# Two-layer graph kernel: the scaled and split diffusion rows of a block moved to the next pair's first attention groups

## The chip, the cores and the metric

The kernel runs on one core of a Trainium2 chip. The metric is the device time of one launch in microseconds. The engines are TensorE (PE in the profile; its weight loads are PEld), VectorE (DVE), ScalarE (ACT), GpSimd (POOL) and SyncE (SP, which here only issues DMAs). Each has its own queue of instructions.

## The reference

Two layers over 2708 nodes with 512 features. The first is a graph attention layer. The second layer, cut to what matters here:

```python
def _adj_from_feats(Xa, W1, W2, W3):
    logits = (Xa @ W1) @ W2 @ (Xa @ W3).T
    # keep, in each row, the fewest largest softmax shares that sum to 0.9
    masked = jnp.where(keep, logits, -jnp.inf)
    return jax.nn.softmax(masked, axis=1)

S = S + eye(n)
Rf = S / S.sum(axis=1, keepdims=True)
Rb = S / S.sum(axis=0)[:, None]
Xf = Xb = Xa = X
Z = 0
for s in range(2):
    A = _adj_from_feats(Xa, W1, W2, W3)
    Xf = Rf @ Xf
    Xb = Rb @ Xb
    Xa = A @ Xa
    Z = Z + (Xf @ U1[s] + Xb @ U2[s] + Xa @ U3[s])
Y = layernorm(X + Z) * gamma + beta
```

In the first step Xf and Xb start from the same X, so that S @ X is computed once; its rows are scaled by the row sums for Xf and by the column sums for Xb.

## The kernel before, in words

Rows are cut into 22 tiles of 128 (the last has 20 rows), two tiles make a pair (11 pairs), four make a quad (6 quads, the last of two tiles). After the first layer the loop `for s in range(STEPS)` does the two steps of the second. Within a step `for g in range(-1, NP)` goes over the pairs, and in one turn of it several pieces of work of different pairs stand side by side:

- **Logits** of pair g + 2 (`Logits.products`, L521): 24 matmuls into PSUM, and ACT copies the 12 chunks into `p` (L523), which has four buffers, those of two pairs.
- **Their exponentials** (`Logits.exp`): the row maxima on DVE (L548), and then 19 small steps, the list `fills`: for each tile two passes of ACT over a row (L553 with half the exponent, L560 in place), then a step of POOL that sets three first points (L565 to L575), an empty step, 12 "looks" (L553: each a pass of ACT over a row) and a last POOL step that makes masses of them.
- **The search** of pair g + 1 (`search`), on DVE: a prologue (L624 to L653), two rounds (L629), then `finish`, which writes `keep` (L806, L808, L730) and ends in a branch (L890). `early` is called behind the first round, and brings the row maxima of pair g + 2; `late` is called ahead of `finish`, and brings the rest of pair g's own work.
- **Attention** of pair g (`attended`): `keep` is transposed on PE in groups of four chunks (L1016), copied by ACT (L1020, tile `at`, two buffers) and multiplied with the values (L1035). A tile has six groups, five of four chunks and one of two, so a pair has twelve, counted by n. The copy of group n + 1 stands ahead of group n's matmuls. From `n >= first` on, which is 3 and in pair 0 is 7, each group also takes steps of `fills` (two up to n = 8, then one), and every group takes steps of `others`.
- **Mixing** of pair g (`mixed`, L1076): the products with U1, U2, U3, each in four k steps, which also take one step of `others` each and, in the first two of them, one of `fills` in three k steps.

The list `others` is what `part` returns. It is the product S @ X for a quad, cut in two: an even g brings the first 11 of the 22 chunks of its sum and an odd g the other 11 (`product`, L967, with the loads of `hl`, three buffers, and `s_r`). With the second half, in the first step, `part` adds eight `scaled` steps, two for each tile of the quad (L977): ACT scales the PSUM tile q into `xe` (four buffers), POOL stores it to `xfb_d` (L978), and `split_rows` splits it on DVE into a high and a low part (L181, L182; tile `split_hl`, two buffers), which POOL stores to `fhl_d` or `bhl_d` (L183). The last quad, of two tiles, has four such steps.

Pair g loads its rows of Xf and Xb from `xfb_d` with `diffused` (L1001, on SP's queue), a step that is put into `others`.

PE, ACT, DVE and SP run their instructions in the order in which the program writes them (`tc.manual_schedule`); POOL's order is the scheduler's. For an odd pair in the first step, the eight scaled steps come last in `others`, so they fall into the groups from n = 8 on and into the first k step of `mixed`, and in DVE's queue they stand between the two rounds of the search of pair g + 1 and its `finish`:

```python
late()
finish(0)
```

In pair 0 the eight scaled steps of quad 0 were left over from the turn before (`left`), and stand ahead of its attention.

Of the kernel before, what the change touches and what calls it, by code (L numbers as in the profile page):

```python
# [53 lines left out]
def kernel(  # L54
# [37 lines left out]
    pairs = [list(range(g, min(g + G, NT))) for g in range(0, NT, G)]  # L92
# [17 lines left out]
    fhl_d = dram.tile([NT * P, 2, D], F32, name="fhl_d")  # L110
    bhl_d = dram.tile([NT * P, 2, D], F32, name="bhl_d")
# [13 lines left out]
    rinv = const.tile([P, NT], F32, name="rinv")  # L125
    cinv = const.tile([P, NT], F32, name="cinv")
# [787 lines left out]
    for s in range(STEPS):  # L914
        last = s == STEPS - 1
        with ExitStack() as st:
# [18 lines left out]
            def values():  # L935
                for t in range(NT):
                    nc.sync.dma_start(out=va[:rows[t], t, :], in_=(xa_d if last else va_d)[cols[t], :])
# [5 lines left out]
            def part(half, b):  # L943

                if b // 2 >= len(quads):
                    return []
                quad = quads[b // 2]  # L950
                first = b % 2 == 0
                w = len(quad) * P
                hl_d = (fhl_d if first else bhl_d) if last else vhl_d
                cs = range(NT) if last else range(0, NT // 2) if first else range(NT // 2, NT)
                steps = []

                def product(c):
                    if c == 0:
                        half[:] = [ps_s.tile([P, D], F32, name=f"q{i}") for i in range(len(quad))]
                    hl = sp.tile([P, 2, D], F32R, name="hl", bufs=3)  # L960
                    nc.sync.dma_start(out=hl.bitcast(F32), in_=hl_d[c * P:(c + 1) * P])
                    s_r = sp.tile([P, 2 * G * P], F32R, name="s_r")
                    nc.sync.dma_start(out=s_r[:, :w].bitcast(F32),
                                      in_=s_d[c * P:(c + 1) * P, quad[0] * P:quad[0] * P + w])
                    for j in range(len(quad)):
                        for h in range(2):
                            nc.tensor.matmul(half[j], lhsT=s_r[:, j * P:(j + 1) * P], rhs=hl[:, h],  # L967
                                             start=(c == 0 and h == 0), stop=(c == NT - 1 and h == 1))

                def scaled(t, ps, i, inv, to):  # L970
                    pr = rows[t]

                    if last and b < 2 and t % 2:
                        x = work.tile([P, D], F32, name="xw", bufs=2)
                    else:
                        x = work.tile([P, D], F32, name="xe", bufs=2 if last else 4)
                    nc.scalar.activation(x[:pr], ps[:pr], AF.Copy, scale=inv[:pr, t:t + 1])  # L977
                    nc.gpsimd.dma_start(out=xfb_d[i, cols[t], :], in_=x[:pr])  # L978
                    if not last:
                        split_rows(parts, nc.vector, x[:pr], t, to)  # L980

                steps += [lambda c=c: product(c) for c in cs]
                if last or not first:
                    for j, t in enumerate(quad):
                        if first or not last:
                            steps.append(lambda j=j, t=t: scaled(t, half[j], 0, rinv, fhl_d))
                        if not first:
                            steps.append(lambda j=j, t=t: scaled(t, half[j], 1, cinv, bhl_d))
                return steps

            def paced(steps, n):
                for step in steps[:n]:
                    step()
                del steps[:n]

            def diffused(grp):
                out_ = []
                for i in range(2):
                    for t in grp:
                        x = work.tile([P, D], F32, name=f"x{i}")  # L1000
                        nc.sync.dma_start(out=x[:rows[t]], in_=xfb_d[i, cols[t], :])  # L1001
                        out_.append(x)
                return out_[:len(grp)], out_[len(grp):]

            def attended(grp, keep, rden, fills, others, then, first=3):

                def turned(i, t, cs):
                    pr = rows[t]
                    pt = ps_t.tile([P, TG, P], F32, name="t")
                    at = work.tile([P, TG, P], F32, name="at")
                    for j, c in enumerate(cs):
                        nc.tensor.transpose(pt[:rows[c], j, :pr], keep[i][:pr, cols[c]], ident[:pr, :pr])  # L1016
                    full = sum(rows[c] == P for c in cs)
                    for r, j0, j1 in ((P, 0, full), (rows[cs[-1]], full, len(cs))):
                        if j0 < j1:
                            nc.scalar.copy(at[:r, j0:j1, :pr], pt[:r, j0:j1, :pr])  # L1020
                    return at

                steps = [(i, t, cs) for i, t in enumerate(grp) for cs in tgroups]
                at = turned(*steps[0])
                xa = []
                total = len(others)
                for n, (i, t, cs) in enumerate(steps):
                    pr = rows[t]
                    nxt = turned(*steps[n + 1]) if n + 1 < len(steps) else then()
                    if n >= first:  # L1030
                        paced(fills, 1 + i if last else 1 if n > 8 else 2)
                    if cs[0] == 0:
                        pa = ps_a.tile([P, D], F32, name="a")
                    for j, c in enumerate(cs):
                        nc.tensor.matmul(pa[:pr], lhsT=at[:rows[c], j, :pr], rhs=va[:rows[c], c, :],  # L1035
                                         start=(c == 0), stop=(c == NT - 1))
                    if not last:
                        paced(others, 1 + i)
                    elif i or len(grp) == 1:
                        paced(others, (total + 10) // 13)  # L1040
                    if cs[-1] == NT - 1:
                        xa.append(work.tile([P, D], F32, name="xa"))
                        nc.scalar.activation(xa[i][:pr], pa[:pr], AF.Copy, scale=rden[:pr, i:i + 1])  # L1043
                        if not last:
                            nc.gpsimd.dma_start(out=xa_d[cols[t], :], in_=xa[i][:pr])
                    at = nxt
                    yield
                return xa, at
# [8 lines left out]
            def turned_rows(grp, v):  # L1057
                return [transposed(up, ps_t, v[i], rows[t], "v_t") for i, t in enumerate(grp)]
# [105 lines left out]
            with tc.manual_schedule(engines={PE, ACT, DVE, SP}):  # L1164
# [4 lines left out]
                steps = lg[0].exp(looks=False)  # L1169
# [4 lines left out]
                half = []  # L1174
                lg += [Logits(pools, s, grp, keys, rank) for grp in pairs[1:2]]
                lg[1].queries()
                for step in part(half, 0):
                    step()
                values()
                done = []  # L1180
                ready = None
                looks, left = [], []
                for g in range(-1, NP):

                    fills = []

                    held = len(left)
                    paced(left, held if last else held // 2)
                    others = left + part(half, g + 2)
                    left = []  # L1190
                    if g == 0 and last:
                        paced(others, 4)
                    if g + 2 < NP:
                        lg[g + 2].products()
                    if g + 3 < NP:
# [3 lines left out]
                    done = []  # L1199

                    rows_in = []
                    if g >= 0:
                        others.insert(0 if g else len(others) // 3, lambda g=g: rows_in.extend(diffused(pairs[g])))
                        final = g == NP - 1 and not last
                        att = attended(pairs[g], *ready, fills, others,
                                       lambda: None if final else turned_rows(pairs[g], rows_in[0]),
                                       3 if g else len(tgroups) + 1)
                    if g == 0:

                        paced(others, held - held // 2 if not last else 0)  # L1210
                        while looks:
                            next(att)
                            paced(looks, 2)

                    def early(g=g):
                        if g + 2 < NP:
# [21 lines left out]
                    if g + 1 < NP:  # L1238
                        ready = search(lg[g + 1], g >= 0, early, late)
# [38 lines left out]
```

## Time and profile before

| | |
|---|---|
| median of 3 runs | 3709.72 us (3704.21 to 3717.26) |
| profiled execution: time | 3708.3 us |
| profiled execution: span | 3706.5 us |
| granted TensorE clock | 0.966 of full speed |
| first step of the second layer | about 1098 to 2301 us of the span |
| second step | about 2301 us to the end |

In a profile's rows, "L977" is a line of the kernel, "q<-hl,s_r" the tile written and those read, and "idle before <-X" the time that the engine stood still before an instruction, with what ended it. A timeline row has the start in us, the duration in us, the engine, the line, the operation and, in brackets, the idle time before it. A row of waits has the waiting engine and line, what it waited for, the total in us, how often, and the longest.

In the first step the products of pair g + 2 (L521) open the turn of pair g. They begin at these times: pair 1 at about 1298, 2 at 1415, 3 at 1522, 4 at 1625, 5 at 1732, 6 at 1834, 7 at 1943, 8 at 2047; pairs 9 and 10 have none, and their attention begins at 2146 and 2227.

### The profile page before, as it was taken

The numbers are of one execution on the slowest core, as the hardware profiler recorded it, in microseconds if no ns is written. First come the engines' busy times: TensorE is split into PE (matmuls) and PEld (weight loads), VectorE is DVE, ScalarE is ACT, GpSimd is POOL, SyncE is SP. The second block draws the span as 40 slices with busy tenths as digits, with TensorE's granted clock in tenths as the row PEclk, the third lists the DMA queues.
The fourth block names the chain that finished last, engine by engine and source line by source line (L and its number), as shares of the span: only waits on it lengthen the run. The fifth ranks groups of instructions, "written<-read, shape, count | busy, mean of one in ns | idle before, by whom it ended". The sixth has DMA issues, their size and how long they took to land. (4 is left out here: it accounts for less than half of the span.)

```text
span 3706.5 us, 35338 instructions
## 1 busy us (share of the span) xinstructions
PE 3367.4 (91%) x11143; PEld 1754.4 (47%) x11143; DVE 2612.9 (70%) x4820; ACT 1541.5 (42%) x2334; POOL 799.6 (22%) x1119
## 2 busy tenths in 40 slices
PE   7998999998966988989899899688999999999898
PEld 4433333333444545545455453445655565556452
DVE  4588888889957637365463651969988779777991
ACT  2343212111114674655666612345654556445511
POOL 4114140514331112121202121302112111121101
PEclk9999999999978999999999999999999999999999
DMA  3477424233228445454535353966556665566552
GB/s 113 152 252 243 137 80 150 80 105 103 74 87 278 164 157 187 145 183 149 205 131 196 128 191 100 302 203 225 175 187 208 233 216 204 183 213 234 201 201 66
DMA packets 276459, 634.08 MB, mean 171 GB/s; under 512 B 37210, under 2 KB 70442, under 8 KB 273244
## 3 DMA queue, kind: packets, MB, share of 16 engines
q1 hardware_dynamic: 249183, 540.99, 44.2%
q0 software_dynamic: 27024, 90.30, 6.3%
q8 instruction: 89, 1.46, 0.2%
q14 instruction: 163, 1.33, 0.1%
HBM read 509.07 MB, written 122.10 MB: 170 GB/s over the span
## 5 line engine op out<-in xcount | busy, mean ns | idle before, releaser
L1035 PE MATMUL a<-va,at 128*128 128x512 f32 (+2 forms) x1936 | 890.1, 599 | 14.0 <-ACT at L1020 13.5
L967 PE MATMUL q<-hl,s_r 128*128 128x512 f32 x2904 | 820.9, 429 | 62.5 <-DMA s_r<-s_d 62.2
L429 PE MATMUL po<-e,fw 128*65 128x512 f32 (+4 forms) x2112 | 838.7, 552 | 34.3 <-DVE e L427 21.8
L427 DVE SCALAR_TENSOR_TENSOR e<-r_b,kk,a_c 128x512 f32<-128x512 f32 (+4 forms) x1056 | 751.8, 741 | 73.5 <-PE po L429 23.7
L967 PEld LDWEIGHTS q<-hl,s_r 128*128 128x128 f32 x2904 | 544.4, 190 | 307.5 <-issue 133.2
L553 ACT ACTIVATE junk_a<-p,nth 128x2708 uint8<-128x2708 f32 (+1 forms) x240 | 613.1, 2554 | 70.6 <-POOL nth L572 66.8
L429 PEld LDWEIGHTS po<-e,fw 128*65 128x65 f32 (+1 forms) x2112 | 286.2, 140 | 546.7 <-issue 269.2
L1035 PEld LDWEIGHTS a<-va,at 128*128 128x128 f32 (+2 forms) x1936 | 337.1, 187 | 379.4 <-issue 342.7
L1076 PE MATMUL a<-u_k,v_t 128*128 128x512 f32 (+1 forms) x1056 | 489.9, 601 | 22.3 <-ACT xa L1043 15.4
L629 DVE SCALAR_TENSOR_TENSOR junk<-p,th 128x2708 bf16<-128x2708 f32 (+1 forms) x132 | 401.2, 3039 | 4.0
L1020 ACT COPY at<-t 128x512 f32<-128x512 f32 (+3 forms) x308 | 140.4, 477 | 494.5 <-PE t L1016 494.1
L1076 PEld LDWEIGHTS a<-u_k,v_t 128*128 128x128 f32 (+1 forms) x1056 | 188.9, 187 | 242.1 <-issue 182.9
L521 PE MATMUL t<-keys,q_t 128*128 128x452 f32 x528 | 167.1, 443 | 118.4 <-ACT p L523 98.1
L181 DVE TENSOR_SCALAR split_hl<-xe 128x512 int32<-128x512 int32 (+1 forms) x44 | 19.1, 434 | 257.1 <-ACT xe L977 210.7
L808 DVE MAX8 vn<-keep 128x8 f32<-128x2708 f32 (+1 forms) x66 | 196.8, 2981 | 2.3
L523 ACT COPY p<-t 128x452 f32<-128x452 f32 (+2 forms) x264 | 132.0, 538 | 126.5 <-PE t L521 82.3
L521 PEld LDWEIGHTS t<-keys,q_t 128*128 128x128 f32 x528 | 91.7, 211 | 189.2 <-ACT p L523 150.7
L411 ACT ACTIVATE s_c<-a_c 128x512 fp32r<-128x512 f32 (+3 forms) x132 | 76.1, 577 | 247.5 <-DMA a_c<-in_adj_t_dram 120.7
L1016 PE MATMUL t<-ident,keep 128*128 128x128 f32 (+1 forms) x968 | 147.2, 274 | 27.1 <-DVE keep L757 19.2
L1016 PEld LDWEIGHTS t<-ident,keep 128*128 128x128 f32 (+1 forms) x968 | 115.0, 139 | 107.5 <-issue 79.5
L548 DVE TENSOR_REDUCE nmx<-p 128x1 f32<-128x2708 f32 (+1 forms) x44 | 129.0, 2966 | 41.7 <-ACT p L523 41.7
L565 POOL TENSOR_TENSOR x<-sums,powers 128x4 f32<-128x4 f32 x22 | 44.7, 2033 | 508.7 <-ACT p L560 508.7
(296 smaller groups left out, 3151.9 us busy)
## 6 DMA issues: line engine op xcount, KB each, us to landing
s_r<-s_d SPq DMA_DIRECT2D x330, 256.0 KB
hl<-vhl_d SPq DMA_DIRECT2D x132, 512.0 KB
u_k<-in_L_gnn_U_dram SPq DMA_DIRECT2D x264, 256.0 KB
hl<-fhl_d SPq DMA_DIRECT2D x132, 512.0 KB
hl<-bhl_d SPq DMA_DIRECT2D x132, 512.0 KB
arow<-in_adj_dram SPq DMA_DIRECT2D x21, 1354.0 KB
s_d<-s_c SPq DMA_DIRECT2D x88, 256.0 KB
a_c<-in_adj_t_dram SPq DMA_DIRECT2D x84, 256.0 KB
```

Source lines behind the costliest of these rows:

```text
L427: nc.vector.scalar_tensor_tensor(e[:pr, :cw], r_b[:pr, i, :cw], kk[:pr, t, hd:hd + 1], a_c[t][:pr, :cw], op0=OP.max, op1=OP.mult)
L429: nc.tensor.matmul(po[i][:, :cw], lhsT=fw[:pr, t, hd, :], rhs=e[:pr, :cw], start=(t == 0), stop=(t == NT - 1))
L521: nc.tensor.matmul(pl[:, :c1 - c0], lhsT=q[:, i], rhs=self.keys[:, c0:c1], start=(i == 0), stop=(i == 1))
L523: nc.scalar.copy(p[:pr, c0:c1], pl[:pr, :c1 - c0])
L553: nc.scalar.activation(junk[:pr], self.p[i][:pr], func, **kw)
L629: v.scalar_tensor_tensor(junk_b[:pr], ps_[i][:pr], th, ps_[i][:pr], op0=OP.is_ge, op1=OP.mult, accum_out=dst)
L808: v.max(vs, keep[0][:pr])
L967: nc.tensor.matmul(half[j], lhsT=s_r[:, j * P:(j + 1) * P], rhs=hl[:, h], start=(c == 0 and h == 0), stop=(c == NT - 1 and h == 1))
L1016: nc.tensor.transpose(pt[:rows[c], j, :pr], keep[i][:pr, cols[c]], ident[:pr, :pr])
L1020: nc.scalar.copy(at[:r, j0:j1, :pr], pt[:r, j0:j1, :pr])
L1035: nc.tensor.matmul(pa[:pr], lhsT=at[:rows[c], j, :pr], rhs=va[:rows[c], c, :], start=(c == 0), stop=(c == NT - 1))
L1076: nc.tensor.matmul(pz[i][:rows[t]], lhsT=v_t[i][:, k, :rows[t]], rhs=u_k, start=(n == 0 and k == 0), stop=(n == 2 and k == KD - 1))
```

## The change

`part` returns two lists, the products and the scaled steps. In the first step the scaled steps of a quad are kept back in `left` until the next turn of the loop. There, for an even pair from 2 on (and for pair 10), they are issued two at a time behind each of the first four attention groups, before the search of the next pair is written. DVE's queue therefore has them behind the end of one search and ahead of the prologue of the next. While they last, the attention takes no other step (`begun` is empty), and `fills` is empty too, since `early` has not been called yet.

The first step's attention takes a product in two groups of three (`1 if n % 3 else 0`), where it took one in each of a pair's first six groups and two in each of the others. `diffused` goes to the third place of the list (in pair 0 behind a third of it), where it was the first. In the second step the lists come out as before.

```diff
                 if b // 2 >= len(quads):
-                    return []
+                    return [], []
...
                 steps += [lambda c=c: product(c) for c in cs]
+                scales = []
                 if last or not first:
                     for j, t in enumerate(quad):
                         if first or not last:
-                            steps.append(lambda j=j, t=t: scaled(t, half[j], 0, rinv, fhl_d))
+                            scales.append(lambda j=j, t=t: scaled(t, half[j], 0, rinv, fhl_d))
                         if not first:
-                            steps.append(lambda j=j, t=t: scaled(t, half[j], 1, cinv, bhl_d))
-                return steps
+                            scales.append(lambda j=j, t=t: scaled(t, half[j], 1, cinv, bhl_d))
+                return steps, scales
...
                     if not last:
-                        paced(others, 1 + i)
+                        paced(others, 1 if n % 3 else 0)
...
-                for step in part(half, 0):
-                    step()
+                for steps in part(half, 0):
+                    paced(steps, len(steps))
...
-                    held = len(left)
-                    paced(left, held if last else held // 2)
-                    others = left + part(half, g + 2)
-                    left = []
+                    if g == 0:
+                        paced(left, len(left) if last else len(left) // 2)
+                    others, scales = part(half, g + 2)
                     if g == 0 and last:
                         paced(others, 4)
+                    if last:
+                        others += scales
+                        scales = []
...
+                    begun = []
                     if g >= 0:
-                        others.insert(0 if g else len(others) // 3, lambda g=g: rows_in.extend(diffused(pairs[g])))
+                        others.insert(len(others) // 3 if g == 0 else 0 if last else 2, lambda g=g: rows_in.extend(diffused(pairs[g])))
                         final = g == NP - 1 and not last
-                        att = attended(pairs[g], *ready, fills, others,
+                        att = attended(pairs[g], *ready, fills, others if last or not g else begun,
                                        lambda: None if final else turned_rows(pairs[g], rows_in[0]),
                                        3 if g else len(tgroups) + 1)
                     if g == 0:
 
-                        paced(others, held - held // 2 if not last else 0)
+                        paced(left, len(left))
                         while looks:
                             next(att)
                             paced(looks, 2)
+                    elif not last:
+
+
+                        while left:
+                            next(att)
+                            paced(left, 2)
+                        begun += others
+                        others = begun
+                    left = scales
```

## The prediction

> **What bounds the kernel now.** I read the page first. TensorE (PE) is busy most, so only gaps on PE, or work that lengthens them, can move the end.
>
> ```profile
> PE 3367.4 (91%) x11143; PEld 1754.4 (47%) x11143; DVE 2612.9 (70%) x4820; ACT 1541.5 (42%) x2334; POOL 799.6 (22%) x1119
> ```
>
> The chain of waits covers only the last 80 us, in the second step, which the edit leaves as it is. So next come the waits in the window 1416 to 2048 us, which is pairs 2 to 7 of the first step (columns: total us, times, longest).
>
> ```profile
> DVE split_hl L181 <- ACT xe L977: 135.7, 6, 42.8
> PE t L521 <- ACT p L523: 31.9, 20, 11.0
> ACT p L523 <- DVEq L890: 24.6, 3, 10.1
> ```
>
> Read backwards: PE waits for ACT to copy logits into `p`; ACT waits for the DVE's branch at the end of a search (L890), which frees those buffers; and DVE sat for 135.7 us before the splits, with that end behind them in its queue. The timelines show one case, pair 3 into pair 4 (DVE, then ACT, then PE; start, duration, idle before).
>
> ```profile
> 1586.65 0.43 DVE L181 TENSOR_SCALAR split_hl<-xe 128x512 int32<-128x512 int32 x1 [42.79 <-ACT xe L977]
> ...
> 1605.65 0.43 DVE L181 TENSOR_SCALAR split_hl<-xe 128x512 int32<-128x512 int32 x1 [2.88 <-DMA bhl_d<-split_hl]
> ...
> 1606.72 3.03 DVE L806 SCALAR_TENSOR_TENSOR keep<-p,th 128x2708 f32<-128x2708 f32 x1
> ...
> 1638.02 0.17 DVE L907 RECIPROCAL rden<-den 128x2 f32<-128x2 f32 x1 [5.18 <-issue]
> ```
>
> ```profile
> 1634.20 0.97 ACT L523 COPY p<-t 128x452 f32<-128x452 f32 x2 [7.09 <-DVEq L890]
> ```
>
> ```profile
> 1634.79 7.52 PE L521 MATMUL t<-keys,q_t 128*128 128x452 f32 x20 [7.92 <-ACT p L523]
> 1642.31 1.28 PE L1016 MATMUL t<-ident,keep 128*128 128x128 f32 x8
> ...
> 1733.85 1.12 PE L521 MATMUL t<-keys,q_t 128*128 128x452 f32 x4 [0.74 <-ACT p L523]
> ```
>
> The last row is the next turn, from an even pair to an odd one: no splits stand before that search's end, and the wait is 0.74. The odd-to-even turns wait 8.20 (pair 1 to 2), 7.92, 10.95 and 6.37 (7 to 8): 33.4 us in all.
>
> **What the Trainium skill says.** "Trainium Architecture — The Big Picture", section Inside one NeuronCore: each engine has its own instruction stream, and they meet only through semaphores. The trace agrees: DVE stood 42.79 us before one split. All my argument rests on such queues. "Perfetto Trace Analysis", Optimization Strategy: find the gaps on the engine concerned and what blocks it; done above, and below for the new order. "DMA: Bandwidth & Descriptors", Anatomy of one DMA — SWDGE (gpsimd) path: about 2.0 us plus bytes over 436 GB/s, an estimate of 3.2 us for a 512 KB split; the trace has a median of 3.5 us from issue to landing in this window, which is what I use.
>
> **The change, part by part.** Let S be the first transposition of a pair (L1016, 1642.31 in pair 4).
>
> *1. Splits out of the odd pairs (1, 3, 5, 7).* DVE's finish no longer stands behind eight scaled steps. It then ends as in an even pair, some 19 us ahead of the turn (rden at 1712.55, products at 1731.66). The four waits of 33.4 us fall to the 0.74 of an even turn: **-30.4 us**. Late next there: only the `p` copies at 0.54 us a chunk, as now. The odd pairs also lose 2.33 us before L1076 (ACT behind with `xa`) and about 1 us for u_k; part 4 takes this back.
>
> *2. Splits into the next even pair (2, 4, 6, 8), ahead of its search.* This puts a new chain on ACT's path. DVE's queue becomes: eight splits, search prologue, first round, the two maxima (L548), second round. ACT's becomes: four groups' copies with the eight xe, copy 5, then exponentials that need the maxima, with copy 6 behind them. From the rows:
> - The first xe follows the copies at0 and at1, which end 1.9 us after S (1643.00 plus 1.21); the first split starts at S+2.5.
> - Eight splits last 20.1 us from 1586.65 to 1606.72, and 18 us in pair 0, where they stand at this place. Their own DVE work is 8 x 1.15 = 9.2; the rest is two buffers, each refilled some 4 us after its last use, the 3.5 us landing. I take 17.8, the shorter, since the xe come early: S+20.3.
> - Prologue, L624 to the first mass: 1638.11 to 1643.08, 5.0. First round, 1643.08 to 1650.12: 7.0. First maximum: 2.97. S+35.2.
> - ACT's two passes over the row, L553 and L560, with their small ones: 2079.14 to 2084.61, 5.5. Copy 6: 0.6. S+41.3.
>
> When does PE want copy 6? A group without a product takes 3.87 (1585.32 to 1589.19), with one 5.72 (1649.02 to 1654.73): a product is 1.84, a short last group (two chunks of rows) without one 2.5. Two transpositions 1.33; four groups without a product to S+16.4; one product 18.2; group 4 with a product, the short transposition ahead of it, 23.7; group 5 (short, with the xfb loads in place of a product) 26.2; transposition 7: S+26.6. So **PE stands 14.7 us**. Before, DVE needed none of this: the maxima ended at 1655.97, S+13.7, ahead of the first pass. After the stall the first pass of the second tile delays copy 7 (2.2), and copy 10 comes after looks of 2.61 each (1.6): 18.5 a pair, 74 for four. Pair 8 has 3.5 us of such waits already (0.63, 1.77, 1.08), which I don't count twice: **+70.5 us**.
>
> *3. DMAs and queues.* Each of the eight steps brings two POOL DMAs of 0.54 us: 16, 8.7 us of POOL, in a stretch where POOL next waits for ACT's exponentials. Nothing, hidden by that wait; uncovered at most 8.7 a pair. SP reads xfb_d at the third place of the list, now soon after it is written; what SP holds behind it are the loads of the third product, wanted two groups later: 0 to 2 us a pair, taken as nothing. PSUM q is read out by S+15, before the next quad's first product at S+16.4: nothing.
>
> *4. Products spread over groups (two in three groups, the rest beside u_k).* In groups 3 to 8 ACT has a copy and two passes, 5.7 us (2102.79 to 2108.48). Before, PE had 5.7 with one product and 7.5 with two; now every third group has 3.87. Pair 8, whose products are half as long, shows what short cover does:
>
> ```profile
> 2108.63 3.70 PE L1035 MATMUL a<-va,at 128*128 128x512 f32 x8 [0.63 <-ACT at L1020]
> 2114.32 3.70 PE L1035 MATMUL a<-va,at 128*128 128x512 f32 x8 [1.77 <-ACT at L1020]
> ```
>
> Laid out for an odd pair I find 0 to 3 us at copies 8 and 10, and some 1.9 before `xa`: as much as the 3.4 that part 1 frees, so **0**, bounds -3.5 to +3 a pair. More products beside u_k ask 1 MB per 3.6 us, near the highest GB/s of the page: 0 to 2 us a pair.
>
> *5. The ends.* Pair 0 already runs four groups ahead of its search, with six steps left over for the turn (13.95 us): unchanged but for spreading, **+1**. Pairs 9 and 10 move four splits to a pair without a search: 0.4 less, nothing counted. The second step's lists come out as before: 0.
>
> Sum: -30.4 + 70.5 + 0 + 1 = +41. The profiled execution had a span of 3706.5 and 3708.3 us; 3749 for it, and 3750 for a median that stood 1.4 above it.
>
> **The rivals.**
> (a) *The turn is gained and ACT never starves* (faster). If the maxima come by about S+21, PE finds copy 6 ready and only part 1 remains, with perhaps 1 to 4 us a pair of part 4: 3708 - 30 + 4 to 16, about 3690. The sign turns where the stall of an even pair is below 7.6 us (30.4 over 4), with copy 6 by about S+34. For it: DVE is idle from some 19 us before the turn, and the splits' own work is 9.2. Against: the first xe cannot precede the pair's first copies, and 15 us of search follow the splits in any case, so S+34 needs splits of under 11 us with two buffers.
> (b) *ACT becomes the bound in every pair* (slower still): 3 to 5 us more in nine pairs, through the thinner cover and late `xa`, and DMA beside u_k: about 3785. For it: pair 8's waits. Against: ACT's share of a pair is near 60 of 105 us.
> (c) *The gain and the loss cancel* within measurement: a stall of 6 to 9 us an even pair, about 3710. A shift of one group in how far PE runs ahead would not do it (3.87); it takes two.
>
> **How the numbers follow.** Forecast 0.70, rival (b) 0.10, (a) 0.13, (c) 0.07. The forecast's own range is 3725 to 3772: splits of 17.8 to 20.1 and 3 us of order in the even pairs (four of them, -10 to +16), part 4's bounds (about 12 either way). Down to 3695 the range takes in (c) and the mild end of (a), up to 3785 most of (b). A difference under 0.3% (11 us) cannot be told from no change here. Faster by more 0.13, within 0.08, slower by more 0.79.
>
> **What would show it.** In the profile after: the odd-to-even wait before L521 near 0.7 instead of 8, and no 42 us wait of DVE ahead of L181 in the odd pairs. In pairs 2, 4, 6 and 8: ACT idle some 16 us before L556, released by DVE's maxima, and PE idle some 15 us before L1035, released by ACT's copy. If that PE gap is under 8 us, step 2 is wrong and with it the sign; if gaps stand in odd pairs before L1035 or L1076 by more than 3 us each, part 4 was too low.

## The result, and the profile after

The changed kernel takes 3762.78 us (median of 4 runs, 3760.02 to 3765.53), the kernel before in the same comparison 3711.39 us (3704.21 to 3717.26). The ratio is 1.0139 with a 95% interval of 1.0119 to 1.0160: slower by 1.4%. The forecast was 3750, slower, with a range of 3695 to 3785. The profiled execution has a span of 3763.7 us (3706.5 before). Lines after 982 of the kernel stand one to thirteen lines further down than before: attention's copy is L1021, its matmul L1036, U's matmul L1077.

The page of the changed kernel first: engine totals, and two groups of section 5 (busy us, mean ns, then idle before them and what ended it).

```profile
PE 3375.4 (90%) x11143; PEld 1758.6 (47%) x11143; DVE 2603.2 (69%) x4820; ACT 1541.4 (41%) x2334; POOL 799.2 (21%) x1119
...
L1036 PE MATMUL a<-va,at 128*128 128x512 f32 (+2 forms) x1936 | 904.3, 607 | 111.3 <-ACT at L1021 111.3
...
L521 PE MATMUL t<-keys,q_t 128*128 128x452 f32 x528 | 161.2, 430 | 87.5 <-ACT p L523 66.9
```

The work is the same (x11143, x4820, x2334), and the busy times hardly move. What moves is idle time of PE: before L1036 it was 14.0 us and is 111.3, before L521 it was 118.4 and is 87.5. The same two groups in the kernel before:

```profile
L1035 PE MATMUL a<-va,at 128*128 128x512 f32 (+2 forms) x1936 | 890.1, 599 | 14.0 <-ACT at L1020 13.5
...
L521 PE MATMUL t<-keys,q_t 128*128 128x452 f32 x528 | 167.1, 443 | 118.4 <-ACT p L523 98.1
```

The waits in the window that the prediction used, 1416 to 2048 us (now pair 2 to the middle of pair 7), say who keeps whom:

```profile
DVE split_hl L181 <- ACT xe L977: 115.5, 3, 38.9
...
PE a L1036 <- ACT at L1021: 76.0, 20, 22.0
...
ACT nmx L556 <- DVE nmx L548: 67.8, 3, 23.7
...
DVE split_hl L181 <- DMA fhl_d<-split_hl: 28.0, 9, 4.7
...
PE t L521 <- ACT p L523: 7.8, 27, 0.7
```

L521 no longer waits longer than 0.7 at one time. In its place PE waits for ACT's copy, and ACT for the row maxima of DVE. Pair 4 shows the chain once: the timelines of DVE, of ACT and of PE.

```profile
1645.87 0.43 DVE L181 TENSOR_SCALAR split_hl<-xe 128x512 int32<-128x512 int32 x1 [38.86 <-ACT xe L977]
...
1668.27 0.43 DVE L181 TENSOR_SCALAR split_hl<-xe 128x512 int32<-128x512 int32 x1 [1.29 <-DMA bhl_d<-split_hl]
...
1674.32 3.04 DVE L629 SCALAR_TENSOR_TENSOR junk<-p,th 128x2708 bf16<-128x2708 f32 x1
...
1681.36 5.84 DVE L548 TENSOR_REDUCE nmx<-p 128x1 f32<-128x2708 f32 x2
```

```profile
1684.36 0.20 ACT L556 ACTIVATE nmx<-nmx 128x1 f32<-128x1 f32 x1 [21.65 <-DVE nmx L548]
...
1689.82 0.56 ACT L1021 COPY at<-t 128x512 f32<-128x512 f32 x1
```

```profile
1636.96 1.12 PE L521 MATMUL t<-keys,q_t 128*128 128x452 f32 x4 [0.74 <-ACT p L523]
...
1643.48 1.09 PE L1017 MATMUL t<-ident,keep 128*128 128x128 f32 x8 [0.20 <-ACT p L523]
...
1690.44 6.55 PE L1036 MATMUL a<-va,at 128*128 128x512 f32 x8 [20.01 <-ACT at L1021]
```

DVE is idle for 38.86 us, then splits until 1669.4, then does prologue, round and maxima. ACT's pass has stood in its queue for 21.65 us, with the copy for group 6 behind it, and PE stands for 20.01 us. Its first eight matmul records after that (two for each of the group's four chunks) last 6.55 us, where other groups have 3.60.

Most readings below rest on the length of a pair, taken as the time from the first L160 of one pair to that of the next in PE's timeline. An even pair so begins with the wait at its turn.

| pair | 1 | 2 | 3 | 4 | 5 | 6 | 7 | 8 | 9 | 10 |
|---|---|---|---|---|---|---|---|---|---|---|
| before, us | 117.2 | 107.0 | 103.3 | 106.3 | 101.9 | 109.5 | 104.3 | 98.8 | 79.9 | 47.7 |
| after, us | 113.7 | 125.7 | 98.9 | 123.7 | 98.9 | 124.6 | 98.9 | 118.5 | 79.1 | 47.7 |

The first step (up to the first L1128, which is L1129 in the changed kernel) ends at 2353.5 us instead of 2301.2. That is 52.3 of the 57.2 us between the spans; the second step took 1410.3 instead of 1405.3, and 1404 to 1409 in the runs below, so that its 5 us may be no more than the scatter between executions.

### The profile page after: what moved, and what is told of

It is laid out like the page before. It is cut to its first block, busy times and chain, and to the rows that moved or that the text cites. A ratio compares the mean times of both kernels' runs of the same rounds, so it can differ in the third digit from the quotient of the medians.

```text
span 3763.7 us, 35370 instructions
## 1 busy us (share of the span) xinstructions
PE 3375.4 (90%) x11143; PEld 1758.6 (47%) x11143; DVE 2603.2 (69%) x4820; ACT 1541.4 (41%) x2334; POOL 799.2 (21%) x1119
## 5 line engine op out<-in xcount | busy, mean ns | idle before, releaser
L1036 PE MATMUL a<-va,at 128*128 128x512 f32 (+2 forms) x1936 | 904.3, 607 | 111.3 <-ACT at L1021 111.3
L967 PE MATMUL q<-hl,s_r 128*128 128x512 f32 x2904 | 833.9, 432 | 65.9 <-DMA s_r<-s_d 65.5
L967 PEld LDWEIGHTS q<-hl,s_r 128*128 128x128 f32 x2904 | 547.4, 191 | 318.9 <-issue 143.4
L1036 PEld LDWEIGHTS a<-va,at 128*128 128x128 f32 (+2 forms) x1936 | 341.9, 189 | 488.2 <-issue 354.9
L1077 PE MATMUL a<-u_k,v_t 128*128 128x512 f32 (+1 forms) x1056 | 488.4, 596 | 6.0 <-ACT xa L1044 5.1
L1021 ACT COPY at<-t 128x512 f32<-128x512 f32 (+3 forms) x308 | 139.7, 476 | 426.5 <-PE t L1017 426.5
L1077 PEld LDWEIGHTS a<-u_k,v_t 128*128 128x128 f32 (+1 forms) x1056 | 188.6, 185 | 205.4 <-issue 172.4
L521 PE MATMUL t<-keys,q_t 128*128 128x452 f32 x528 | 161.2, 430 | 87.5 <-ACT p L523 66.9
L521 PEld LDWEIGHTS t<-keys,q_t 128*128 128x128 f32 x528 | 87.4, 202 | 156.8 <-ACT p L523 115.8
L806 DVE SCALAR_TENSOR_TENSOR keep<-p,th 128x2708 f32<-128x2708 f32 (+1 forms) x44 | 133.4, 3032 | 28.8 <-PE t L1017 27.2
```

The source lines that it names most:

```text
L521: nc.tensor.matmul(pl[:, :c1 - c0], lhsT=q[:, i], rhs=self.keys[:, c0:c1], start=(i == 0), stop=(i == 1))
L806: v.scalar_tensor_tensor(keep[0][:pr], ps_[i][:pr], t, ps_[i][:pr], op0=OP.is_lt, op1=OP.mult, accum_out=left[:pr, i:i + 1] if e else None)
L1077: nc.tensor.matmul(pz[i][:rows[t]], lhsT=v_t[i][:, k, :rows[t]], rhs=u_k, start=(n == 0 and k == 0), stop=(n == 2 and k == KD - 1))
```

## The experiments

Theory A is the prediction's: in pairs 2, 4, 6 and 8, PE starves because ACT's first pass over a row waits for maxima that stand behind the splits on DVE. The rivals are the thinner cover by products (B), the splits' length as such, which would only move the wait to the turn (C), and, for the length of the stall, the DMA traffic beside the splits (D) or the stores alone (E). All experiments are edits of the changed kernel. Ratios are to the kernel before, with 95% intervals; the other numbers are from the profiled executions. The before has a median for each of three comparisons: the changed kernel's, the next four runs', the last four runs'.

| run | median, us | ratio | pair 4 / 5, us | first step ends |
|---|---|---|---|---|
| before | 3711.4, 3708.1, 3708.8 | 1 | 106.3 / 101.9 | 2301.2 |
| after | 3762.8 | 1.0139 (1.0119 to 1.0160) | 123.7 / 98.9 | 2353.5 |
| old pacing | 3743.7 | 1.0097 (1.0080 to 1.0113) | 122.7 / 97.6 | 2335.6 |
| maxima first | 3682.1 | 0.9936 (0.9919 to 0.9952) | 104.5 / 98.9 | 2272.1 |
| splits behind round and maxima | 3689.8 | 0.9952 (0.9935 to 0.9968) | 106.6 / 98.8 | 2279.5 |
| row loads later | 3736.9 | 1.0077 (1.0060 to 1.0094) | 116.2 / 100.7 | 2327.7 |
| maxima first, old pacing | 3649.0 | 0.9834 (0.9820 to 0.9849) | 98.0 / 97.6 | 2238.2 |
| the same, row loads later | 3655.0 | 0.9847 (0.9833 to 0.9862) | 99.2 / 97.6 | 2251.2 |
| splits behind maxima, old pacing | 3663.3 | 0.9869 (0.9851 to 0.9886) | 102.8 / 97.6 | 2256.2 |
| old pacing, row loads later | 3707.3 | 0.9995 (0.9988 to 1.0001) | 113.4 / 97.7 | 2300.7 |

### Old pacing alone

```diff
-                        paced(others, 1 if n % 3 else 0)
+                        paced(others, 1 + i)
```

> The changed kernel with one part undone: the attention's products are paced as before (1 + i a group) while the scaled steps stay at their new place. Theory A (the loss is the stall of PE in pairs 2, 4, 6 and 8, where ACT's first pass over a row waits for row maxima that stand behind the splits on DVE): the 20 to 23 us gaps before L1036 stay, only the gaps of 1 to 2 us at groups 8 to 10 go, so 3750 to 3765 us. Rival B (the thinner cover by products is the loss, ACT binds the groups): the time falls by 30 us or more, to near 3720.

Measured: 3743.65 us. The stall stays, here in pair 4 on PE's timeline (the row counts only the matmuls up to 1690 us, so x5 is not the whole group; the same holds for the rows of L1036 below with fewer than eight):

```profile
1685.86 4.63 PE L1036 MATMUL a<-va,at 128*128 128x512 f32 x5 [21.33 <-ACT at L1021]
```

So B is not the main cause. But the first step is 17.9 us shorter, and the time lies six under A's range: the thin pacing costs 1.0 to 1.6 us in each odd pair and 1.0 to 5.5 in each even one. It is a second cost of its own.

### Row maxima ahead of the splits

```diff
                     begun = []
+                    first_ = []
...
                     elif not last:
...
+                        if left and g + 2 < NP:
+                            first_ = lg[g + 2].exp()
                         while left:
...
-                            fills.extend(lg[g + 2].exp())
+                            fills.extend(first_ or lg[g + 2].exp())
```

`first_` is an empty list in the other pairs. The maxima are issued when `exp` is called, the 19 steps go into `fills` at the old place.

> The changed kernel, with the row maxima of pair g + 2 issued on DVE ahead of the eight splits in pairs 2, 4, 6 and 8; prologue and first round stay behind the splits. Theory A: the maxima are there when ACT asks, the four gaps of 20 to 23 us (86 us in all) go, and the time is 3670 to 3690 us, below the kernel before. Rival B (pacing): at most 20 us less than the changed kernel. Rival C (the splits' own length and their stores at that place make the search late, whatever stands behind them): the gap moves to the turn before L521, and the time stays above 3740.

Measured: 3682.07 us, 81 less than the changed kernel and below the kernel before. DVE and then PE in pair 4:

```profile
1617.79 2.97 DVE L548 TENSOR_REDUCE nmx<-p 128x1 f32<-128x2708 f32 x1 [32.15 <-ACT p L523]
1621.70 2.97 DVE L548 TENSOR_REDUCE nmx<-p 128x1 f32<-128x2708 f32 x1 [0.93 <-ACT p L523]
1624.59 0.42 DVE L181 TENSOR_SCALAR split_hl<-xe 128x512 int32<-128x512 int32 x1
...
1647.54 0.43 DVE L181 TENSOR_SCALAR split_hl<-xe 128x512 int32<-128x512 int32 x1 [2.79 <-DMA bhl_d<-split_hl]
```

```profile
1648.07 3.60 PE L1036 MATMUL a<-va,at 128*128 128x512 f32 x8
1653.00 3.70 PE L1036 MATMUL a<-va,at 128*128 128x512 f32 x8 [0.90 <-ACT at L1021]
```

The maxima now lie in DVE's idle time ahead of the splits. The splits are as long as in the changed kernel (23.8 to 24.5 us), and prologue and first round still follow them, yet group 6 starts at 1648.07 with no wait, and the turn to the next pair waits 0.72. That is A; C falls, since the long splits by themselves cost PE nothing. What is left in even pairs (104.5 against 98.9) are waits of 3.2 to 5.0 us at one later copy: the thin pacing.

### First four groups and splits behind the first round and the maxima

```diff
-                    elif not last:
...
-                        while left:
-                            next(att)
-                            paced(left, 2)
-                        begun += others
-                        others = begun
+                    late_s = []
+                    if g > 0 and not last:
+                        if g + 1 == NP:
+                            while left:
+                                next(att)
+                                paced(left, 2)
+                        else:
+                            late_s = left
                     left = scales
...
                             fills.extend(lg[g + 2].exp())
+                        if g > 0 and not last:
+                            while late_s:
+                                next(att)
+                                paced(late_s, 2)
+                            begun.extend(others)
+                            others[:] = []
...
```

> The changed kernel, with the first four groups and the eight splits issued behind the first round and the row maxima of the next search instead of ahead of its prologue. DVE's idle 39 us ahead of the first split can then hold prologue and first round. Theory A: as for maxima first, 3665 to 3690 us, with no gap over 3 us before L1036. Rival C: the splits now stand between the rounds, the search ends later relative to the pair, and a wait before L521 comes back; above 3700 us.

Measured: 3689.82 us, at the edge of A's range, and with waits that A had excluded. PE in pair 4:

```profile
1643.91 0.73 PE L967 MATMUL q<-hl,s_r 128*128 128x512 f32 x2 [2.51 <-ACT xe L977]
...
1666.28 4.11 PE L1036 MATMUL a<-va,at 128*128 128x512 f32 x5 [3.61 <-ACT at L1021]
```

The turn still waits 0.7, so C isn't seen. The longest wait at a copy is 7.4 us, in pair 8. `fills` is now filled when group 3 is issued, and two of its passes (1637.1 to 1642.7 us in pair 4) stand on ACT ahead of the last two xe; the next quad's first product waits for these. Going ahead with prologue and round as well as with the maxima gained nothing.

### Loads of the scaled rows later

```diff
-                        others.insert(len(others) // 3 if g == 0 else 0 if last else 2, lambda g=g: rows_in.extend(diffused(pairs[g])))
+                        others.insert(len(others) // 3 if g == 0 else 0 if last else 5, lambda g=g: rows_in.extend(diffused(pairs[g])))
```

> The changed kernel, with the loads of the scaled rows (diffused) at the sixth place of the list instead of the third. In the changed kernel the eight splits of pair 4 last 23.4 us instead of the 17.8 that the forecast took, and their stores land in 5.0 to 5.5 us instead of 3.5, while SP's loads of those rows and of the next products stand in the same stretch. Theory D (these loads lengthen the stores' landing): landing near 4 us, splits of 19 to 21 us, the gap before L1036 3 to 4 us smaller in each of four pairs, 3745 to 3752 us. Rival E (the stores crowd each other, the loads have no part): landing and time as in the changed kernel, 3758 to 3766 us.

Measured: 3736.93 us, a larger gain than D named. The DMA view of the stretch of pair 4's splits (issues, KB each, median us to landing), the changed kernel first and then this one:

```profile
xfb_d<-xe POOLq DMA_DIRECT2D x8, 256.0 KB, 5.1
fhl_d<-split_hl POOLq DMA_DIRECT2D x4, 512.0 KB, 5.0
bhl_d<-split_hl POOLq DMA_DIRECT2D x4, 512.0 KB, 5.5
```

```profile
xfb_d<-xe POOLq DMA_DIRECT2D x8, 256.0 KB, 3.2
fhl_d<-split_hl POOLq DMA_DIRECT2D x4, 512.0 KB, 3.8
bhl_d<-split_hl POOLq DMA_DIRECT2D x4, 512.0 KB, 3.8
```

The eight splits fall from 23.6 to 17.7 us; the first and the last of this run, and then PE's wait in pair 4:

```profile
1640.54 0.43 DVE L181 TENSOR_SCALAR split_hl<-xe 128x512 int32<-128x512 int32 x1 [39.24 <-ACT xe L977]
...
1657.13 0.43 DVE L181 TENSOR_SCALAR split_hl<-xe 128x512 int32<-128x512 int32 x1
```


```profile
1679.32 5.27 PE L1036 MATMUL a<-va,at 128*128 128x512 f32 x8 [12.31 <-ACT at L1021]
```

Of the 7.7 us that this gap loses, 5.9 are the splits and 1.8 a product that now stands in group 5 in place of the loads. In the changed kernel SP reaches the loads early, waits for the stores of xe, and then brings 1 MB of rows and three products' operands (0.75 MB each) into the very stretch in which the splits wait for their stores. With the edit the queue of SP's loads moves 0.96 MB in this stretch, where it moved 3.24. D holds, E falls; whether the rows or the products' operands count more, no run separates. Odd pairs lose 1.8 us (100.7), with waits of 0.96 and 1.75 at two copies.

### Two or three of these together

Old pacing with the maxima first:

> Row maxima ahead of the splits, and the products paced as before (1 + i). The old pacing alone took 18 us off the first step, the maxima alone 81. Theory A with the pacing as a second, separate cost: the two add up, 3660 to 3668 us. If the maxima had already taken the pacing's cost with them: 3680 us as with the maxima alone.

Measured: 3649.02 us, 1.7% below the kernel before and the fastest of all; 11 us under the range of "the two add up". The waits of PE from 1200 to 2230 us, nearly the whole first step:

```profile
PE t L521 <- ACT p L523: 24.5, 36, 14.0
PE a L1036 <- ACT at L1021: 7.2, 12, 2.8
```

Of the 24.5, 13.96 stand at pair 0's turn. The even pairs take 98.0 us, as long as an odd one. The two cures exceed their sum because the pacing could show only part of its cost while the stall stood before it: the 3 to 5 us waits with the maxima first are what the old pacing covers.

The same with the row loads later:

> As the run before, and the loads of the scaled rows at the sixth place. With the maxima ahead, the splits no longer stand between PE and its next copy. Theory A: their length costs nothing now, so shorter splits (18 us instead of 24) leave the time as in the run before within 4 us, 3658 to 3668. If the DMA traffic of this stretch costs PE something by another way (copies or products late), 8 to 12 us less.

Measured: 3654.95 us, 6 more, where A allowed 4, though the splits fell to between 16.6 and 18.3 us; the two intervals overlap. Of the difference in the profiles, 6.3 us are there when pair 1 begins (1298.7 against 1292.4), where the edit has not moved any work yet, so these may be scatter; 4.7 arise in pair 8, where copy 9 is 5.3 us late, and why there only is left open. So no gain: once the maxima are ahead, the splits' length is off PE's path.

The splits behind the maxima with the old pacing:

> First four groups and splits behind the first round and the maxima, with the old pacing. Alone it was 8 us slower than the maxima ahead, with a gap of 2.5 us at the first product of the next quad (ACT's last xe) and 3.3 to 7.4 us at one copy. Theory A: the pacing covers the copy's gap and the gap at the product stays: 3666 to 3676 us, 5 to 10 above the run with the maxima ahead.

Measured: 3663.30 us, 3 under A's range, and 14 above the maxima first with the old pacing, where A named 5 to 10. The 2.51 us at L967 stays, and a wait of 4.4 us at one copy of pair 8 with it.

Old pacing and later row loads, with the maxima still behind the splits:

> The changed kernel with the old pacing and the loads of the scaled rows at the sixth place, the maxima still behind the splits. The two took 18 and 26 us off alone. Theory A and D: the gap before L1036 stays at 11 to 14 us in the four even pairs, since prologue, round and maximum (15 us) follow the splits whatever their length; the sum is 3715 to 3725 us, still above the kernel before. If DMA traffic were the whole cause of the stall, the gap would be under 5 us and the time under 3700.

Measured: 3707.26 us, as fast as the kernel before (0.9995) and 8 below A's range. The gap is what prologue, round and maximum leave even behind splits of 17.8 us:

```profile
1668.67 3.78 PE L1036 MATMUL a<-va,at 128*128 128x512 f32 x4 [12.35 <-ACT at L1021]
```

The gaps of the four even pairs are 12.6, 12.4, 11.5 and 16.0 us; the last lies above A's 11 to 14. So DMA traffic explains some 7 us of pair 4's stall (the splits last 17.8 us here and 24.9 with the old pacing alone), and not the 12 that stay.

## Why the prediction was right, and where its terms were off

**Direction and mechanism held.** The gap, its place and its chain are those of step 2: after the fifth copy ACT stands until DVE's maxima, and PE before group 6.

**Step 1, turns: right.** 33.4 us became four times 0.74: -30.5 measured, -30.4 forecast. The odd pairs gained besides: -3.5, -4.4, -3.0 and -5.4 us in pairs 1, 3, 5 and 7, 16.3 together. The forecast had their 3.4 us taken back by step 4; two of the four, pairs 3 and 7, lie beyond its bound of -3.5. In these two the wait of 2.33 us before U's matmul was followed by slow matmuls in the kernel before (the last section), another 1.6 to 1.7 us, and these went with it. The pacing took back only the 1.0 to 1.6 a pair that the old pacing regained.

**Step 2, the stall: right in kind, short in size.** Counted from S = 1643.48 in pair 4:

| | forecast | measured |
|---|---|---|
| first split | S+2.5 | S+2.4 |
| eight splits, us | 17.8 | 23.6 (23.6 to 25.6 in the four pairs) |
| first maximum done | S+35.2 | S+40.8 |
| PE wants copy 6 | S+26.6 | S+27.0 |
| PE's gap, us | 14.7 | 20.0 (20.0 to 23.1) |

The mis-sized term is the splits' length. It took the stores' landing from the kernel before, 3.5 us, where such loads did not stand beside them (SP's loads moved 0.32 MB from 1584 to 1608 us, around pair 3's splits, and 3.24 MB from 1640 to 1672 us in the changed kernel), and it was 5.3 (median of pairs 2 to 8). The fault is in **step 3**, which priced SP's loads in that stretch at nothing because their own user wanted them late, and did not ask what they do to the stores. With the loads later the splits last 17.7. Its other term held: q is read out at S+15.1, and the next quad's first product did not wait. Without the 30.5 us of the turns, the four even pairs grew by 101.4 us where 70.5 stood: 27 more in the gaps themselves (86.0 against 58.8), some 9.5 in slow matmuls after them, and some 6 less in the smaller waits that follow.

**Step 4, pacing: too low.** Forecast 0 net; the old pacing takes 17.9 us off the first step, most of it in even pairs, which that step had laid out for an odd pair only.

**Step 5: right.** Pair 0's turn keeps its 13.96, pairs 9 and 10 move by 0.8 and 0.

The sum: even pairs +101.4 - 30.5, odd pairs -16.3, the ends -2.2, which is +52.4, against 52.3 measured in the first step. Of the ends, 1.3 us are there before the second layer begins and are not the change's. That +41 came nearer than its terms is luck: the odd pairs' unforeseen gain hid part of the even pairs' excess of 31 us. The forecast's own range is not the plain sum of its parts either: -10 to +16 and 12 either way give 3728 to 3778 around 3750, where it says 3725 to 3772.

**The rivals.** Rival (a), faster, needed copy 6 by S+34, and the splits in under 11 us; they never came below 16.6. It came true in another way that the prediction did not see: the maxima need not stand behind the splits at all. Its turning point of a stall of 7.6 us is wrong for the old pacing, where stalls of 11.5 to 16.0 us only just balance the gains, since the odd pairs gain 4.2 to 6.7 us each besides the turns. Rival (b) was part of the truth, at 18 us instead of 35.

## What to carry to other kernels

When work is moved from behind one engine's wait to an idle stretch, list what follows it in that queue and who needs that first: here 9 us of splitting were cheap, and the 6 us of row maxima behind them were what another engine's whole queue hung on. Put the instruction that others wait for ahead of the bulk, and give slack to the bulk. And take a transfer's time from a stretch with the traffic that the new place will have.

## What the runs showed of the hardware that was not expected

After each of the four gaps of 20 us or more, the first matmul record of group 6 lasts 1220 ns, the next two to five 1061 and, after one between, the later ones 592; from start to start that is 853 ns instead of 430. A group of eight so takes 5.1 to 6.4 us from start to start where it has 3.0 to 3.5 otherwise: 1.6 to 3 us more for each stall, which the prediction did not price. The clock that the trace shows as granted to PE tells the same. Around pair 4's gap it is 1.00 up to 1672.3 us, 0.50 from there to 1696.2, and 1.00 again; PE's last matmul ended at 1670.4 (the profile's ends of matmuls are modelled) and the first after the gap began at 1690.4.

"TensorE: Matmul & The Clock Gate" of the Trainium skill, Part 1: The HAM clock gate, describes a clock that is halved after an idle window of about 3.4 us until activity has lasted as long. The trace agrees in the halving, and in the order of the recovery, which came 3.1 to 5.8 us after the four gaps ended. It does not agree with 3.4 us of idleness as the condition: in the four gaps the clock fell 1.2 to 1.9 us after PE's last matmul, and three gaps of 2.33 to 2.40 us (before U's matmul in pairs 3 and 7 of the kernel before, at a copy in pair 8 of the changed one) were followed by 0.50 too, while those of 2.33 us in pairs 1 and 5 before were not. What decides between them is open.

The landing of 512 KB stores went with the other loads beside them. The medians were 3.6 and 3.7 us around pair 3's splits in the kernel before, where the core's DMA moved 265 GB/s over 24 us; 3.8 in pair 4 with the row loads later, 266 GB/s over 28 us; and 5.0 and 5.5 in pair 4 of the changed kernel, 303 GB/s over 32 us. SP's loads were 0.32, 0.96 and 3.24 MB of that.
